# Layer values between the MLP's second products, later exps and work moved off VectorE, in a fused two-layer graph kernel

## The chip, the cores and the metric

The kernel runs on one core of one Trainium2 chip. The metric is the device time of one execution in microseconds (us). Instructions of a core are issued by five engines: TensorE (PE in the profile; its weight loads are shown apart as PEld), VectorE (DVE), ScalarE (ACT), GpSimd (POOL) and SyncE (SP), which issues most of the DMAs. In this kernel the order of each engine's instructions is fixed when the program is built, and an engine waits at the first instruction whose inputs or buffers are not ready.

## What is computed

Sixteen graphs (batches) of 1024 nodes with 256 features go through two layers. `adj` is symmetric with ones on its diagonal.

```python
# layer 0: attention over neighbours (8 heads of 32, q = k = v), then an MLP
h = relu(layernorm(x))
n = layernorm(h) * gamma1 + beta1                # split into 8 heads
p = softmax(where(adj > 0, n @ n.T / sqrt(32), -inf))
h = h + p @ n
y = layernorm(h) * gamma2 + beta2
x = x + h + gelu(y @ W1 + b1) @ W2 + b2
# layer 1: one head over neighbours
f = relu(layernorm(x));  g = f @ W
e = leaky_relu((g @ a_1).T + g @ a_2 + (g @ a_12) @ g.T, 0.2)
a = softmax(where(adj > 0, e, -9e15))
x = x + elu(f @ W_1 + (a @ f) @ W_2)
```

## The kernel before

**Two chains at once.** The Python code that builds the program runs several generators ("streams") against a common scale of places and always advances the one that is furthest behind. Stream A is the attention of batch b. Stream B is everything after the attention of batch b−1: MLP, layer 1 and the store. The other streams prepare the next batch: C loads and normalizes it, M loads masks, K compares masks, P makes the first MLP inputs. Each stream's instructions thus land between the others', on every engine in the same order.

**Stream A.** For b > 0 a batch has 24 units, numbered 0 to 23 here. A unit is one key tile (128 keys) for one group of four heads and one half (512) of the queries. `scores` makes the scores of the four heads (TensorE, `s`, L994), adds the mask on VectorE in two instructions of 128x1024 (L1007), and takes the exps on ScalarE in four instructions of 128x512 that also sum their rows (`weights`, L1014). `go_on` then lets TensorE multiply the exps of the unit before with the values (`weigh`, `o`, L1109), and adds 2.0 to the planner's clock. Units 0 to 15 are for the first half of the queries; in every second one (the even ones) `mirror` also transposes the exps (VectorE, L1030), writes them to DRAM and adds up their columns on GpSimd (`add_up`, L1043), so that units 16 to 23 can read the mirrored blocks back instead of computing them (`weigh_mirrored`, L1091). The first two heads' exps are issued in `scores`, the other two after `go_on`.

**Deferred work.** `defer(us, f)` puts an instruction aside until the planner's clock has moved on by `us`; `run_deferred`, called after every step of a stream, issues what is due, in order of due time. The clock is an estimate of TensorE time: 2.0 for a unit, 0.5 for a transpose to PSUM ("turn"), 1.75 or 0.9 for a piece of stream B.

**Turns.** `ask(turn, c)` puts a turn into a list; `make_turns` issues what is in the list ahead of the next unit. `wait_for(turn, c)` holds stream B until that turn has been issued.

**Stream B.** It is cut into pieces of 1.75 (some 0.9) clock units, some three to a unit of A, in this order: `expand(0)`; the last attends of the batch before; `expand(1)`, `contract(0)`, `expand(2)`, `contract(1)`, `expand(3)`, `contract(2)`, `contract(3)`; then layer 1. Here c = 0..3 is a chunk of 256 nodes, two tiles of 128. `expand` is the MLP's first product (TensorE `ph`, ScalarE `hid` L1303, four pieces) and `contract` its second (TensorE `po`, added to the rows by VectorE, L1327; four pieces, two for each tile). `prepare1` takes a finished chunk's statistics (VectorE `st_d`, L741 to L744, then GpSimd `rs_d`, L746) and defers its normalization (`ft`, VectorE L750) by 5.0; `turn1` issues that normalization if it has not been issued yet, transposes the chunk (`ptf`, L1349) and lets ScalarE write it into `fT` (L1352). Layer 1 then has `project_half` (`puT`, evicted by ScalarE, L1364), `values` (`pg`, one for each of 8 tiles, evicted into `gw` by ScalarE for even tiles and VectorE for odd ones, L1379), `weights` (`lg`, VectorE L1397 and L1402, ScalarE exp L1403) and `attend` (`pf`, `pa`).

**Buffers.** All PSUM results of stream B and all turns go through one ring of three banks, `psm`. A `po` tile stays open over its two pieces. The outputs `o` of the attention have a single bank, `pso`. The scores have two pairs of banks.

**Normalizations.** `normalize` (L750, VectorE) is called for the attention's values (`nrm`), for the MLP's input (`y`, in `prepare`) and for layer 1 (`ft`). The output `o` of a unit group is copied out of PSUM by VectorE (`os`, L1118).

Of the kernel before, what the change touches and what calls it, by code (L numbers as in the profile page):

```python
# [495 lines left out]
def fast_path(  # L496
# [28 lines left out]
    nc = tc.nc  # L525
# [10 lines left out]
    TPH = QW // P  # L536
# [209 lines left out]
        nc.gpsimd.tensor_tensor(rs, ve, mhalf[:, :nt], op=ALU.pow)  # L746
        return mv, rs

    def normalize(dst, src, mv, rs, t):
        nc.vector.tensor_scalar(  # L750
            dst, src, mv[:, t, 0:1], rs[:, t : t + 1], op0=ALU.subtract, op1=ALU.mult
        )

# [5 lines left out]
    def defer(us, f):  # L759
        deferred.append((clock[0] + us, len(deferred), f))  # L760

        return clock[0] + us
# [13 lines left out]
    def prologue(b, st):  # L776
# [33 lines left out]
        def value(i):  # L810
            mv, rs = stats["b", i]
            for j in range(TPC):
                t = i * TPC + j
                nrm = tmpp.tile([P, D], F32, tag="w1", bufs=6, name=f"nrm_{b}_{t}")
                normalize(nrm, h[t // TPH][:, t % TPH, :], mv, rs, j)
                nc.gpsimd.tensor_mul(nrm, nrm, g1)
                nc.gpsimd.tensor_add(va[:, t, :], nrm, be1)

# [149 lines left out]
    def attention(b, st):  # L968
# [9 lines left out]
        def scores(qh, g, kt):  # L978
            qs = slice(qh * QW, (qh + 1) * QW)
            sc = [  # L980
                psc.tile([P, 2, QW], F32, tag=f"sc{i}", name=f"s_{b}_{g}_{qh}_{kt}_{i}") for i in range(2)
            ]

            by_pe = 2 if b == 0 else 0
            if by_pe:
                for j in range(by_pe):
                    matmul(
                        sc[j // 2][:, j % 2, :], ident8, st[qh][:, kt // 2, :, kt % 2], start=True, stop=False
                    )
                clock[0] += 0.45  # L990
            for j in range(GH):
                r = slice(j * HD, (j + 1) * HD)
                for c in range(0, P, P // 2):
                    nc.tensor.matmul(  # L994
                        sc[j // 2][c : c + P // 2, j % 2, :],
                        kT[r, g, kt * P + c : kt * P + c + P // 2],
                        kT[r, g, qs],
                        start=j >= by_pe,
                        stop=True,
                    )  # L1000
            mb = st[qh][:, kt // 2, :, kt % 2].unsqueeze(1).to_broadcast([P, 2, QW])
            es = []
            for i in range(2):
                e = ep.tile([P, 2, QW], F32, tag="e", name=f"e_{b}_{g}_{qh}_{kt}_{i}")
                masked = sc[i]
                if 2 * i >= by_pe:
                    nc.vector.tensor_tensor(e, masked, mb, op=ALU.add)  # L1007
                    masked = e
                es.append(e)

                def weights(e=e, masked=masked, i=i):
                    for j in range(2):
                        n = 2 * i + j
                        nc.scalar.activation(  # L1014
                            e[:, j], masked[:, j], AF.Exp, scale=SCALE,
                            accum_out=sums[kt // TPH, g][:, n, kt % TPH, qh : qh + 1],
                        )

                if i == 0:
                    weights()  # L1020
            return es, weights


        def mirror(g, kt, es):
            x = xp.tile([P, NT // 2 * GH, GH, HD], F32, tag="x", name=f"x_{b}_{g}_{kt}")
            if g not in blocks:
                blocks[g] = dramp.tile([NT // 2 * GH, NT // 2 * GH, HD, P], F32, tag=f"blocks{g}", name=f"blocks_{b}_{g}")

            def turn(i):
                nc.vector.transpose(  # L1030
                    x[:, :, 2 * i : 2 * i + 2, :].rearrange("p c h j -> p h c j"),
                    es[i].rearrange("p h (c i) -> p h c i", i=HD),
                )

            def write():
                for a in range(GH):
                    nc.sync.dma_start(
                        blocks[g][(kt - TPH) * GH + a].rearrange("c i e -> i c e"),
                        x[a * HD : (a + 1) * HD].rearrange("p c h j -> p c (h j)"),
                    )  # L1040

            def add_up():
                add = lambda out, p, q: nc.gpsimd.tensor_tensor(out, p, q, op=ALU.add)  # L1043
                part = denp.tile([P, TPH * GH, GH, 8], F32, tag="part", bufs=1, name=f"part_{b}_{g}_{kt}")
                add(part, x[:, :, :, 0:8], x[:, :, :, 8:16])
                add(part, part, x[:, :, :, 16:24])
                add(part, part, x[:, :, :, 24:32])
                add(part[:, :, :, :4], part[:, :, :, :4], part[:, :, :, 4:])
                add(part[:, :, :, :2], part[:, :, :, :2], part[:, :, :, 2:4])
                row = denp.tile([P, GH, TPH, GH], F32, tag="row", name=f"row_{b}_{g}_{kt}")  # L1050
                add(
                    row.rearrange("p a t h -> p t a h"),
                    part[:, :, :, 0].rearrange("p (t a) h -> p t a h", a=GH),
                    part[:, :, :, 1].rearrange("p (t a) h -> p t a h", a=GH),
                )
                if ("rows", g) not in blocks:
                    blocks["rows", g] = dramp.tile([TPH, P, GH * TPH * GH], F32, tag=f"rows{g}", name=f"rows_{b}_{g}")
                defer(7.0, lambda: nc.sync.dma_start(blocks["rows", g][kt - TPH], row.rearrange("p a t h -> p (a t h)")))

            defer(1.5, lambda: turn(0))  # L1060
            defer(3.5, lambda: turn(1))
            defer(5.5, write)
            defer(6.5, add_up)

        def gather(g):
            r = blocks["sums", g] = denp.tile([P, NT // 2 * GH, TPH * GH], F32, tag="sums", bufs=1, name=f"gather_{b}_{g}")
# [37 lines left out]
        def weigh(qh, g, kt, es, first, last):  # L1104
            if first and not (mirrored and qh == 1):
                acc[g, qh] = pso.tile([P, QW], F32, tag="o", name=f"o_{b}_{g}_{qh}")
            o = acc[g, qh]
            for j in range(GH):
                nc.tensor.matmul(  # L1109
                    o[j * HD : (j + 1) * HD, :],  # L1110
                    va[:, kt, (g * GH + j) * HD : (g * GH + j + 1) * HD],
                    es[j // 2][:, j % 2, :],
                    start=first and not (mirrored and qh == 1),
                    stop=last,
                )
            if last:
                c = os[g, qh] = tmpp.tile([P, QW], F32, tag="w2", bufs=5, name=f"os_{b}_{g}_{qh}")
                nc.vector.tensor_copy(c, o)  # L1118
                if qh == NQH - 1:
                    close(qh, g)  # L1120

# [88 lines left out]
    def prepare(b, st, c):  # L1210

        h = hs[b]
        assert finished[b, c // 2] == NG
        ts = range(c * TPC, (c + 1) * TPC)
        mv, rs = norm_stats([h[t // TPH][:, t % TPH, :] for t in ts], f"c{b}_{c}")

        def apply():
            y = tmpp.tile([P, TPC, D], F32, tag="y", name=f"y_{b}_{c}")
            for i, t in enumerate(ts):
                normalize(y[:, i, :], h[t // TPH][:, t % TPH, :], mv, rs, i)  # L1220
            st["y", c] = y, None

        st["y", c] = None, defer(5.0, apply)
# [8 lines left out]
    def rest(b, st, tails):  # L1232
# [4 lines left out]
        def load(c):  # L1237
            for t in range(c * TPC, (c + 1) * TPC):
                xt.append(xbp.tile([P, D], F32, tag="xb", name=f"xb_{b}_{t}"))
                nc.sync.dma_start(xt[t], rows(x, b, t))  # L1240
# [180 lines left out]
        def attend(t, es):  # L1421
# [32 lines left out]
            defer(14.0, lambda: nc.sync.dma_start(rows(out, b, t), z))  # L1454
            yield 1.75, True

        load(0)
        ask(turn, 0)
        yield
# [18 lines left out]
        prepare1(1)  # L1478
        fT = st["fT"] = midp.tile([P, DC, N], F32, tag="mid1", name=f"fT_{b}")
        ask(turn1, 0)  # L1480
        yield from contract(2, hid[2])
        prepare1(2)
        ask(turn1, 1)
        yield from contract(3, hid[3])
        uT = midp.tile([P, DC, N], F32, tag="mid2", name=f"uT_{b}")
        prepare1(3)
        ask(turn1, 2)
# [1 line left out]
        def some_values(*ts):  # L1489
            for t in ts:  # L1490
                values(t, fT)
                yield 0.9, t % 2 == 1
# [11 lines left out]
        yield from wait_for(turn1, 0)  # L1504
        yield from wait_for(turn1, 1)
        yield from project_half(0, 0)
        yield from some_values(0, 1)
        if b < B - 1:
            ask(turn1, 3)
        yield from project_half(0, 1)  # L1510
        yield from some_values(2, 3)
        if b == B - 1:
            ask(turn1, 3)
        yield from wait_for(turn1, 2)
        yield from some_values(4, 5)
        yield from some_weights(0, 0, 1)
        yield from wait_for(turn1, 3)
        yield from project_half(1, 0)
        yield from project_half(1, 1)
        yield from some_values(6, 7)  # L1520

        before = None
        for c in range(NCH):
# [186 lines left out]
```

## Time and profile before

| what | us |
|---|---|
| median of three runs (3427.57 to 3433.45) | 3429.52 |
| the profiled execution's own time | 3435.34 |
| its span, first to last instruction | 3433.2 |
| ScalarE busy, mean over the span | 1966.2 (57%) |
| one batch in the middle: from the first unit of one batch (1608.9) to that of the next (1818.7) | 209.8 |
| exps of a unit on ScalarE, unit 0 of that batch (1613.76 to 1616.33) | 2.57 |
| a piece of stream B with 32 matmul records, spacing in the timeline | 1.73 |
| scores and weighting of a unit on TensorE | 1.04 and 1.00 |

A busy share is an average over the span, and stages differ. All batches but the first and the last have the same order, so one batch in the middle stands for them; a wait that occurs 14 times in the list of waits is one that each such batch has. Times of the timeline are us from the span's start.

### The profile page before, as it was taken

To read this page: it belongs to the slowest core of one execution; us is meant where nothing else is said; L and a number is where in the kernel's file an instruction comes from. 1 tells how busy PE (TensorE), PEld (TensorE's weight loads), DVE (VectorE), ACT (ScalarE), POOL (GpSimd) and SP (SyncE) were. 2 spreads that over 40 slices of the span, in tenths; PEclk is the share of its full clock that TensorE was granted. 3 is DMA by queue.
4 is the path that set the end of the run, shared out by engine and by line. 5 is a ranking of instruction groups with operands and counts; after the bars stand their busy time and mean duration, and the time that the engine had idled before them with its cause. 6 is when DMAs were issued, how large, how long until landed. Compare 5 with 4: busy or idle time off the path is not lost. (4 is left out here: it accounts for less than half of the span.)

```text
span 3433.2 us, 114690 instructions
## 1 busy us (share of the span) xinstructions
PE 3239.3 (94%) x48866; PEld 1590.8 (46%) x48866; DVE 2791.5 (81%) x5201; ACT 1966.2 (57%) x4744; POOL 1535.2 (45%) x1758
## 2 busy tenths in 40 slices
PE   6899999999999999999999999999999999999998
PEld 1344444444444444444444444444444444444477
DVE  6788888888888888887888888888888888887844
ACT  6765745647456474655646556475564745646442
POOL 3553553535535254462545526355353554525220
PEclk9999999999999999999999999999999999999999
DMA  5245455464555545555454555545546445554510
GB/s 134 58 115 157 94 121 125 114 158 99 133 121 122 140 109 121 127 120 144 113 134 112 122 138 119 139 109 125 126 113 158 99 121 132 116 143 101 132 38 14
DMA packets 741158, 404.81 MB, mean 118 GB/s; under 512 B 173216, under 2 KB 699936, under 8 KB 740640
## 3 DMA queue, kind: packets, MB, share of 16 engines
q1 hardware_dynamic: 740352, 397.14, 47.9%
q8 instruction: 386, 6.32, 0.8%
q14 instruction: 132, 1.08, 0.1%
q10 hardware_dynamic: 288, 0.26, 0.0%
HBM read 233.97 MB, written 146.54 MB: 111 GB/s over the span
## 5 line engine op out<-in xcount | busy, mean ns | idle before, releaser
L1014 ACT ACTIVATE e<-e 128x512 f32<-128x512 f32 x1504 | 928.5, 619 | 839.7 <-DVE e L1007 837.5
L1007 DVE TENSOR_TENSOR e<-s,mk 128x1024 f32<-128x1024 f32 x752 | 885.1, 1216 | 204.1 <-PE s L994 197.5
L574 PE MATMUL ph<-yT,w 128*32 128x256 f32 x7808 | 445.8, 379 | 16.4 <-DVE yT L1279 15.0
L574 PE MATMUL pa<-gw,e 128*32 128x258 f32 x7584 | 446.4, 380 | 9.1 <-DVE e L1397 9.1
L574 PE MATMUL lg<-fT,uT 128*32 128x256 f32 x7680 | 452.3, 380 | 0.0
L994 PE MATMUL s<-kT 32*64 32x512 f32 x6272 | 447.0, 622 | 1.1 <-DVE e L1007 1.1
L574 PE MATMUL po<-w,hid 128*32 128x256 f32 x7680 | 434.4, 379 | 0.0
L1109 PE MATMUL o<-e,va 128*32 128x512 f32 x3136 | 428.8, 614 | 1.4 <-ACT e L1014 1.4
L574 PEld LDWEIGHTS ph<-yT,w 128*32 128x32 f32 x7808 | 250.4, 110 | 220.2 <-DVE yT L1279 32.5
L574 PEld LDWEIGHTS po<-w,hid 128*32 128x32 f32 x7680 | 250.0, 110 | 202.7 <-issue 48.5
L574 PEld LDWEIGHTS lg<-fT,uT 128*32 128x32 f32 x7680 | 248.5, 110 | 200.2 <-issue 29.7
L574 PEld LDWEIGHTS pa<-gw,e 128*32 128x32 f32 x7584 | 247.5, 110 | 196.0 <-issue 22.1
L1043 POOL TENSOR_TENSOR part<-part,x 128x512 f32<-128x512 f32 x240 | 309.3, 1289 | 18.8
L1030 DVE STREAM_TRANSPOSE x<-e 128x1024 f32<-128x1024 f32 x240 | 291.5, 1232 | 9.9 <-ACT e L1014 8.2
L966 POOL TENSOR_TENSOR h<-h,ot 128x512 f32<-128x512 f32 x64 | 82.1, 1282 | 455.3 <-DVE ot L962 455.3
L1397 DVE SCALAR_TENSOR_TENSOR e<-lg,gw,mk 128x256 f32<-128x256 f32 x512 | 222.9, 476 | 72.3 <-PE lg L574 62.3
L1014 ACT ACTIVATION_READ_ACCUMULATOR e<-e 128x1 f32 x1504 | 281.1, 187 | 0.0
L1403 ACT ACTIVATE e<-e,shift 128x512 f32<-128x512 f32 x256 | 183.1, 716 | 150.8 <-DVE e L1402 141.1
L1303 ACT ACTIVATE hid<-ph,b1c 128x256 f32<-128x256 f32 x512 | 203.6, 465 | 83.7 <-PE ph L574 61.3
L1043 POOL TENSOR_TENSOR part<-x 128x512 f32<-128x512 f32 x120 | 155.3, 1294 | 208.6 <-DVE x L1030 151.2
L919 POOL TENSOR_TENSOR odd<-mk,mq 128x512 bf16<-128x512 fp8e5 x192 | 236.2, 1237 | 20.9 <-DVE uneven L926 18.7
L1109 PEld LDWEIGHTS o<-e,va 128*32 128x32 f32 x3136 | 63.2, 108 | 327.4 <-issue 212.8
(143 smaller groups left out, 4380.4 us busy)
## 6 DMA issues: line engine op xcount, KB each, us to landing
blocks<-x SPq DMA_DIRECT2D x480, 256.0 KB, 4.7
em<-blocks SPq DMA_DIRECT2D x240, 512.0 KB, 5.0
adj<-in_adj_dram SPq DMA_DIRECT2D x248, 256.0 KB, 4.1
h<-in_x_dram SPq DMA_DIRECT2D x64, 256.0 KB, 4.2
xb<-in_x_dram SPq DMA_DIRECT2D x128, 128.0 KB, 3.4
out_dram<-z SPq DMA_DIRECT2D x128, 128.0 KB, 4.1
rows<-row SPq DMA_DIRECT2D x120, 32.0 KB, 2.6
gather<-rows SPq DMA_DIRECT2D x120, 32.0 KB, 3.3
```

The source lines that it names most:

```text
L574: nc.tensor.matmul(out[c : c + HD], lhsT[:, c : c + HD], rhs, start=start, stop=stop)
L919: nc.gpsimd.tensor_tensor(odd.rearrange("p (u v x) -> p u v x", u=2, v=2), key.rearrange("p (u v x) -> p u v x", u=2, v=2), query.rearrang ...
L966: nc.gpsimd.tensor_add(ho, ho, ot.rearrange("p t j d -> p t (j d)"))
L994: nc.tensor.matmul(sc[j // 2][c : c + P // 2, j % 2, :], kT[r, g, kt * P + c : kt * P + c + P // 2], kT[r, g, qs], start=j >= by_pe, stop= ...
L1007: nc.vector.tensor_tensor(e, masked, mb, op=ALU.add)
L1014: nc.scalar.activation(e[:, j], masked[:, j], AF.Exp, scale=SCALE, accum_out=sums[kt // TPH, g][:, n, kt % TPH, qh : qh + 1],)
L1030: nc.vector.transpose(x[:, :, 2 * i : 2 * i + 2, :].rearrange("p c h j -> p h c j"), es[i].rearrange("p h (c i) -> p h c i", i=HD),)
L1043: add = lambda out, p, q: nc.gpsimd.tensor_tensor(out, p, q, op=ALU.add)
L1109: nc.tensor.matmul(o[j * HD : (j + 1) * HD, :], va[:, kt, (g * GH + j) * HD : (g * GH + j + 1) * HD], es[j // 2][:, j % 2, :], start=first ...
L1303: nc.scalar.activation(hid[:, f0 + i, :], ph[:, i, :], AF.Identity, bias=b1c[:, f0 + i : f0 + i + 1])
L1397: nc.vector.scalar_tensor_tensor(e[:, j, :], lg[:, j, :], gw[:, kt, D : D + 1], st[c // 2][:, kt // 2, qs, kt % 2], op0=ALU.add, op1=ALU.add,)
L1403: ready = defer(2.5, lambda: nc.scalar.activation(e, e, AF.Exp, bias=shift))
```

## The change

- `normalize` gets an argument for its engine. The attention's values (`nrm`, for b > 0) and the MLP's input (`y`) are normalized by GpSimd instead of VectorE; `ft` stays on VectorE.
- For b > 0 all four exps of a unit are deferred by 2.5 in the planner's clock instead of being issued in and right after `scores`. A unit advances the clock by 2.0, so they come after the next piece of stream B and what this piece issues on ScalarE. In `mirror` the due times of the transposes, the write and the sums go up by 1.9 to 2.1.
- The copy `os` goes from VectorE to ScalarE.
- The `values` of tiles 0 and 1 are issued inside `contract(2)`, each after a tile's two pieces, those of tiles 2 and 3 inside `contract(3)`. Layer 1's start is ordered anew: the two first `project_half` follow each other, and the values of tiles 4 to 7 stand singly between `weights` and `project_half`.

```diff
-    def normalize(dst, src, mv, rs, t):
-        nc.vector.tensor_scalar(
+    def normalize(dst, src, mv, rs, t, engine=nc.vector):
+        engine.tensor_scalar(
             dst, src, mv[:, t, 0:1], rs[:, t : t + 1], op0=ALU.subtract, op1=ALU.mult
         )
...
-                normalize(nrm, h[t // TPH][:, t % TPH, :], mv, rs, j)
+                normalize(nrm, h[t // TPH][:, t % TPH, :], mv, rs, j, nc.gpsimd if b else nc.vector)
...
-                if i == 0:
+                if b > 0:
+                    defer(2.5, weights)
+                elif i == 0:
                     weights()
-            return es, weights
+            return es, weights if b == 0 else lambda: None
...
-            defer(1.5, lambda: turn(0))
-            defer(3.5, lambda: turn(1))
-            defer(5.5, write)
-            defer(6.5, add_up)
+            defer(3.6, lambda: turn(0))
+            defer(5.4, lambda: turn(1))
+            defer(7.4, write)
+            defer(8.5, add_up)
...
-                nc.vector.tensor_copy(c, o)
+                nc.scalar.copy(c, o)
...
-                normalize(y[:, i, :], h[t // TPH][:, t % TPH, :], mv, rs, i)
+                normalize(y[:, i, :], h[t // TPH][:, t % TPH, :], mv, rs, i, nc.gpsimd)
...
+        def with_values(pieces, c):
+            for i, piece in enumerate(pieces):
+                yield piece
+                if i % 2 == 1:
+                    yield from wait_for(turn1, c)
+                    values(c * TPC + i // 2, st["fT"])
+                    yield 0.9, i // 2 == 1
...
-        yield from contract(2, hid[2])
+        yield from with_values(contract(2, hid[2]), 0)
         prepare1(2)
         ask(turn1, 1)
-        yield from contract(3, hid[3])
+        yield from with_values(contract(3, hid[3]), 1)
...
         yield from project_half(0, 0)
-        yield from some_values(0, 1)
         if b < B - 1:
             ask(turn1, 3)
         yield from project_half(0, 1)
-        yield from some_values(2, 3)
         if b == B - 1:
             ask(turn1, 3)
         yield from wait_for(turn1, 2)
-        yield from some_values(4, 5)
-        yield from some_weights(0, 0, 1)
+        yield from some_values(4)
+        yield from some_weights(0, 0)
+        yield from some_values(5)
+        yield from some_weights(0, 1)
         yield from wait_for(turn1, 3)
         yield from project_half(1, 0)
+        yield from some_values(6)
         yield from project_half(1, 1)
-        yield from some_values(6, 7)
+        yield from some_values(7)
```

## The prediction

> **What bounds the kernel now.** I read the page's busy table first, then who TensorE waits for, then one batch in time order, then the windows of its stages.
>
> ```profile
> PE 3239.3 (94%) x48866; PEld 1590.8 (46%) x48866; DVE 2791.5 (81%) x5201; ACT 1966.2 (57%) x4744; POOL 1535.2 (45%) x1758
> ```
>
> TensorE is the bound: the span is its 3239.3 us and 194 us of waits. The change takes no matmul away, so only the waits can go. From the list of waits of TensorE (total us, times, longest):
>
> ```profile
> PE ptf L1349 <- ACT uT L1364: 26.1, 14, 1.9
> PE o L1091 <- DMA em<-blocks: 22.9, 19, 2.3
> PE pg L574 <- ACT gw L1379: 20.6, 14, 1.5
> PE ptk L824 <- POOL va L817: 20.5, 6, 15.5
> PE pg L574 <- ACT uT L1364: 18.7, 15, 1.3
> PE ptk L824 <- ACT uT L1364: 18.4, 14, 1.3
> PE ph L574 <- DVE yT L1279: 15.0, 12, 2.0
> ...
> PE o L1091 <- DVE os L1118: 10.2, 13, 0.8
> PE pa L574 <- DVE e L1397: 9.1, 14, 0.7
> ```
>
> Four of these, 26.1 + 20.6 + 18.7 + 18.4 = 83.8 us, are one place in each of 14 batches, the start of layer 1. The timeline of TensorE shows it:
>
> ```profile
> 1712.85 2.22 PE L574 MATMUL pg<-wo,fT 128*32 128x258 f32 x32 [1.48 <-ACT gw L1379]
> 1716.94 0.66 PE L1349 MATMUL ptf<-ident,ft 128*128 128x128 f32 x4 [1.86 <-ACT uT L1364]
> 1717.52 1.11 PE L994 MATMUL s<-kT 32*64 32x512 f32 x16
> ...
> 1732.48 1.08 PE L574 MATMUL pg<-wo,fT 128*32 128x258 f32 x16 [1.30 <-ACT uT L1364]
> 1734.88 0.63 PE L824 MATMUL ptk<-ident,va 128*128 128x128 f32 x4 [1.32 <-ACT uT L1364]
> ```
>
> A `pg` takes 0.86 us and a bank of the ring of three, so a pair of them runs the ring round before ScalarE, busy with exps, has emptied it: 1.48 + 1.86 us up to unit 13 (its scores are the third line), 1.30 + 1.32 up to unit 15, together 5.96. The stages, from unit 0 to 9, 9 to 13, 13 to 15, and 15 to the next batch:
>
> ```profile
> 1608.90:1681.50 72.60, 71.31 (x1165) 35.05 (x1164) 59.19 (x90) 50.88 (x118) 41.80 (x49) 1.00 0.39 85
> 1681.50:1717.50 36.00, 32.33 (x472) 14.86 (x468) 33.50 (x78) 21.41 (x49) 19.38 (x24) 1.00 0.62 144
> 1717.50:1735.40 17.90, 15.28 (x213) 6.22 (x212) 15.74 (x26) 9.81 (x25) 12.64 (x14) 1.00 0.41 78
> 1735.40:1818.70 83.30, 79.81 (x1303) 40.09 (x1303) 68.44 (x136) 39.35 (x101) 25.00 (x28) 1.00 0.65 162
> ```
>
> Columns after the length: busy us of PE, PEld, DVE, ACT, POOL. What matters is the second row: in those 36.00 us VectorE is busy for 33.50, more than TensorE's 32.33. The average of 81% hides that. This is exactly where the change puts the `values`.
>
> [...] `ft` on VectorE has median 411 ns and maximum 1446, and two of them from 1701.18 took 2.44 us while GpSimd ran `part`. [...] no row here shows a one-input tensor_scalar on GpSimd. From above it is bounded by the two-input rows of that size, 0.885 (`nrm`) and 0.742 (`va`). I take 0.65[...].
>
> **Part by part.**
>
> *Normalizations.* These groups leave VectorE (mean ns, total us):
>
> ```profile
> L750 DVE TENSOR_SCALAR y<-h,mv_c,rs_c 128x256 f32<-128x256 f32 x128 | 92.2, 763 | 0.1
> ...
> L750 DVE TENSOR_SCALAR nrm<-h,mv_b,rs_b 128x256 f32<-128x256 f32 x128 | 47.9, 416 | 2.7 <-POOL rs_b L746 2.6
> ...
> L1118 DVE COPY os<-o 128x512 f32<-128x512 f32 x64 | 43.5, 680 | 0.6 <-PE o L1109 0.6
> ```
>
> VectorE loses 92.2 + 120 x 0.416 + 43.5 = 186 us; GpSimd gains 248 x 0.65 = 161 us[...], going from 45% to 50%. Neither is TensorE's time by itself. `nrm` (10 us or more ahead of its `ptk`) and `y` of chunks 0, 1, 3 have slack. The tight one is chunk 2: its `y` may queue behind `add_up` (5.9 us, here 1640.54 to 1646.4) and end near 1648; its transposes run at 1649.7. Cost 0, up to 1.5 us a batch if a mask comparison (1.24) gets in between.
>
> *`os` on ScalarE.* The unit that ends a group has its mask additions (2.35 us) ahead of `os` on VectorE; on ScalarE nothing is left in front of it, since the exps of the unit before are done. The 0.8 us wait of `o` L1091 goes: 10.2 / 14 = -0.73 a batch. ScalarE gains 64 x about 0.67 (the 128x512 `uT` row), hidden in its 43% idle time.
>
> *Later exps.* After a unit's start: scores 1.04, weighting 1.00, a piece 1.73, its eviction 0.84, exps 2.57 make 7.2 us. The weighting that needs them begins no earlier than the shortest unit distance, 7.2, plus 1.04. Margin 1.1 us; the GELU (4.5 us with both table loads) is due at 3.0, after the exps at 2.5, so it stays behind them. Cost 0, at most 1 us a batch. Its own gain is 0 too: the waits above on ScalarE are all in the stage that is rebuilt anyway. What counts is the shift of the transposes: those of unit 8 were both ahead of unit 9's masks; now the second (due 7.4 after unit 8's start; the clock at unit 9 is 7.25) comes behind them, 1.23 us of VectorE more in the full stage.
>
> *Values and the new order.* A unit of A passes for each 5.32 of stream B's 134 clock units (25.2 widths a batch). `contract(2)` begins at B's 50.8, 0.30 of a unit after unit 9. Counting pieces from there, stream B now issues: before unit 10 two halves of `po`; then pg, po, po, pg, po; unit 11: po, pg, po; unit 12: po, pg, puT, puT; unit 13: pg, lg, pg, lg; unit 14: puT, pg, puT; unit 15: pg, lg, lg. No two `pg` follow each other, and after unit 13 I find every bank free in time: in the worst place, before the `pg` of tile 7, the copy of tile 6 ends about half a us early. So the 1.30 + 1.32 go.
>
> Before unit 13 it is different. `turn1` of chunks 2 and 3 both fall ahead of unit 13 (both asked for after unit 12), and the second forces `ft` of chunk 3 onto VectorE at once. Its chain starts at the last `po`: add, statistics, `rs_d`, `ft`. TensorE has only pg 0.86 + puT 1.72 + puT 1.72 + ptf 0.58 = 4.9 us to fill; before it was over 12 us (1702.5 to 1716.94), of which VectorE took 11 (`ft` was done at 1713.6). So VectorE's whole queue from unit 9 to this `ft` now ends before unit 13 can begin. It was 33.50 us of work plus 1.4 us of small gaps from 1682.63 on. It loses a pair of `nrm` (-0.64), gains the transposes of unit 8 (+1.23), and I add 0.8 for idling where a shorter lead makes it wait on TensorE (`ptos` of unit 12, between 0 and 1.7). `ft` ends at 1682.63 + 33.50 + 1.4 + 0.59 + 0.8 = 1718.9, unit 13 starts 0.3 later, 1719.2 against 1717.52: +1.7 us, for the same amount of stream B done. On the way the stalls show as `po` and `puT` waiting for a bank (a `po` that closes one `pg`, 0.86 us, before its bank is needed again) and `ptf` waiting for `ft`. From both sides: +0.9 with no extra idling; +5 if mask conversions and `ft` meet GpSimd's longer queue at each collision (1.7 us for the pair seen at 1701) with full idling.
>
> *Sum a batch:* +1.7 - 2.62 - 0.73 = -1.65; fourteen batches -23 us. The last batch's tail has no units beside it; its early turn costs under 1 us. 3435.34 becomes 3412; the median of the runs lies 5.8 below the profiled one, so 3429.5 becomes 3407.
>
> **Rivals.**
> *Full gain (0.17).* VectorE, 186 us lighter, keeps up, and all of the 83.8 + 10.2 us goes: 3335. For it: the average. Against: only 0.64 of the 186 us leave the stage that is full.
> *Slower (0.28).* The chain into chunk 3's `ft` is longer than reckoned[...]: GpSimd runs `add_up`, then normalizations, while VectorE converts masks and makes `ft`. It decides from the point where unit 13 comes over 3.35 us later than before (2.62 + 0.73). At +5 each batch loses 1.65, +23 us: 3453. For it: 2.44 us for two `ft`. Against: GpSimd is busy 19.38 of the 36 us, so it has room.
> *The exps do harm or nothing.* A weighting that waits for its exps would show as `o` L1109 behind `e` L1014 (1.4 us in all now). I hold it inside the other cases.
>
> **How the numbers follow.** Forecast 0.55, its own range 3380 to 3435; full gain 0.17, slower 0.28. The range 3355 to 3455 leaves out most of the full gain and the far end of the slower case. A measurement of this kernel tells 0.2%, 7 us, from no change. The forecast's case is faster by more with 0.74, the same with 0.16, slower with 0.10. Faster: 0.55 x 0.74 + 0.17 = 0.58; same: 0.09 and 0.02 of the slower case, 0.11; slower 0.31.
>
> **What would show it.** Right: `pg` waits on `gw` and `uT` nearly gone; `o` L1091 on `os` gone; in their place `ptf` on VectorE's `ft`, and `po` or `puT` on VectorE's `xb`, some 4 us a batch; VectorE near full from unit 9 to 13, near 76% in the mean; `o` L1109 on `e` still near zero. Wrong: no new waits of TensorE on VectorE (full gain), or `pty` waiting for GpSimd's `y`, or weightings waiting for exps.

## The result and the profile after

| | before | after |
|---|---|---|
| median of the runs, same chip, us | 3428.77 | 3519.42 |
| ratio, 95% interval | 1 | 1.0262 (1.0246 to 1.0279) |
| span of the profiled execution, us | 3433.2 | 3519.4 |
| its mean granted TensorE clock | 0.993 | 0.982 |

The changed kernel is 91 us slower. From its page, the busy line:

```profile
PE 3276.0 (93%) x48866; PEld 1617.3 (46%) x48866; DVE 2674.6 (76%) x4889; ACT 2001.1 (57%) x4808; POOL 1854.3 (53%) x2006
```

TensorE has the same 48866 matmuls, yet is busy for 36.7 us longer (3239.3 before): some of them run slower. VectorE lost 117 us, not the 186 that were reckoned, and GpSimd gained 319, not 161. Who TensorE waits for after the change (total us, times, longest):

```profile
PE ptf L1351 <- DVE ft L750: 57.7, 30, 4.8
PE o L1093 <- DMA em<-blocks: 31.9, 35, 2.6
PE puT L574 <- DVE xb L1329: 24.5, 13, 2.0
PE ptk L824 <- POOL va L817: 24.2, 6, 15.8
PE pa L574 <- DVE e L1399: 23.9, 16, 1.7
PE ptos L960 <- DVE xb L1329: 19.0, 14, 1.4
...
PE lg L574 <- DVE e L1399: 7.6, 13, 0.6
...
PE o L1111 <- ACT e L1014: 2.2, 1, 2.2
```

(Lines after L1016 stand two higher than before.) The waits of `pg` and `ptk` on ScalarE's `gw` and `uT`, 83.8 us, are gone. In their place stand `ptf` on `ft`, `puT` and `ptos` on `xb`: 101.2 us, all on VectorE, all ahead of unit 13. The weightings do not wait for the later exps (last line). One batch in the order of time, TensorE (start, duration, in brackets the wait before it):

```profile
1749.14 0.65 PE L960 MATMUL ptos<-ident,os 128*128 128x128 f32 x4 [1.43 <-DVE xb L1329]
...
1758.02 1.92 PE L574 MATMUL puT<-fT,wm 128*32 128x512 f32 x16 [1.88 <-DVE xb L1329]
1759.88 0.66 PE L1351 MATMUL ptf<-ident,ft 128*128 128x128 f32 x4
1763.78 0.48 PE L1351 MATMUL ptf<-ident,ft 128*128 128x128 f32 x2 [3.25 <-DVE ft L750]
1764.95 0.69 PE L1351 MATMUL ptf<-ident,ft 128*128 128x128 f32 x2 [0.69 <-DVE ft L750]
1765.57 2.01 PE L994 MATMUL s<-kT 32*64 32x512 f32 x16
1767.51 1.94 PE L1111 MATMUL o<-e,va 128*32 128x512 f32 x8
1769.22 1.84 PE L574 MATMUL pg<-wo,fT 128*32 128x258 f32 x16
```

`ptf` of chunk 3 waits 3.25 us for its `ft`, as the slower case of the prediction had it. The lines below it show what no case had: unit 13's scores take 2.01 us (1.11 at other units), its weighting 1.94 (1.07), `pg` 1.84 (1.05). Windows of the same batch; columns: length, busy us of PE, PEld, DVE, ACT, POOL, granted clock (the share of TensorE's full speed), DMA share, GB/s. The rows are the stages from unit 9 to 13, 13 to 15, 15 to the next batch, and 0 to 9:

```profile
1724.83:1765.57 40.74, 32.89 (x473) 14.95 (x469) 37.99 (x78) 22.75 (x54) 25.54 (x29) 0.98 0.51 122
1765.57:1782.24 16.67, 16.67 (x197) 6.17 (x196) 11.58 (x20) 7.91 (x21) 10.76 (x13) 0.84 0.32 69
1782.24:1868.01 85.77, 81.10 (x1313) 41.90 (x1312) 68.58 (x128) 42.44 (x109) 37.25 (x37) 1.00 0.62 157
1652.55:1724.83 72.28, 71.08 (x1162) 35.11 (x1161) 51.36 (x82) 50.64 (x116) 45.70 (x52) 1.00 0.40 90
```

Around the 3.25 us wait, TensorE alone, in stretches of 3.41 us (length, busy us, granted clock, DMA share, GB/s):

```profile
1757.16:1760.58 3.42, 2.51 (x20) 1.00 0.53 163
1760.58:1763.99 3.41, 0.21 (x2) 1.00 0.00 0
1763.99:1767.40 3.41, 2.72 (x20) 0.50 0.79 162
1767.40:1770.82 3.42, 3.42 (x32) 0.50 0.86 188
1770.82:1774.23 3.41, 3.41 (x68) 1.00 0.24 48
```

After a stretch in which TensorE worked for 0.21 us, its clock is halved for two stretches, 6.83 us: it is still at half after one with 2.72 us of work, and full again after one with 3.42. TensorE was not idle for a whole stretch each time: the paragraph "When the clock drops" below shows a halving after a stretch with 1.48 us of work.

Stage lengths as the mean of the 14 middle batches, from the starts of the units' scores, against the prediction's terms. The `pg` of tile 7 (0.87 us) now stands behind unit 15's start instead of ahead of it; the last column is corrected for it:

| stage | before | after | forecast | slower rival | measured |
|---|---|---|---|---|---|
| 0 to 9 | 71.90 | 71.93 | 0 | 0 | +0.03 |
| 9 to 13 | 36.18 | 41.00 | +1.7 | +5 | +4.82 |
| 13 to 15 | 18.76 | 16.31 | -2.62 | -2.62 | -1.58 |
| 15 to next | 83.05 | 86.08 | -0.73 | -0.73 | +2.16 |
| batch | 209.90 | 215.31 | -1.65 | +1.65 | +5.41 |

Fourteen times 5.41 is 76 of the span's 86 us; the other 10 are outside these batches.

So three questions: what fills VectorE up to unit 13, what the half clock costs, and where the 2.16 after unit 15 come from. VectorE's and then GpSimd's timeline in that stage:

```profile
1746.42 2.33 DVE L594 TENSOR_SCALAR mq<-adj 128x512 fp8e5<-128x512 int32 x2
...
1755.82 1.81 DVE L594 TENSOR_SCALAR mq<-adj 128x512 fp8e5<-128x512 int32 x2
...
1759.69 1.25 DVE L1032 STREAM_TRANSPOSE x<-e 128x1024 f32<-128x1024 f32 x1
...
1762.10 1.24 DVE L1032 STREAM_TRANSPOSE x<-e 128x1024 f32<-128x1024 f32 x1
1763.26 1.63 DVE L750 TENSOR_SCALAR ft<-xb,mv_d,rs_d 128x256 f32<-128x256 f32 x2
```

```profile
1745.76 2.70 POOL L1045 TENSOR_TENSOR part<-part,x 128x512 f32<-128x512 f32 x2
...
1750.18 1.23 POOL L750 TENSOR_SCALAR nrm<-h,mv_b,rs_b 128x256 f32<-128x256 f32 x1
...
1755.84 1.51 POOL L966 TENSOR_TENSOR h<-h,ot 128x512 f32<-128x512 f32 x1
```

Two pairs of mask conversions (L594) take 2.33 and 1.81 us where the median of one is 0.42: each pair runs beside GpSimd instructions that read two tiles (2.70 and 1.51 us in the timeline above). The rest of the trace of the changed kernel agrees: the 99 conversions that no GpSimd instruction overlaps take 428 ns at most, the 61 that only the mirror's sums (L1045) overlap take 852 in the mean. Both transposes of a unit stand ahead of the `ft` that TensorE waits for. L594 alone on VectorE, unit 9 to 13 (length, busy us, clock, DMA share, GB/s), before:

```profile
1681.48:1717.52 36.04, 2.79 (x6) 1.00 0.62 143
```

and after:

```profile
1724.83:1765.57 40.74, 5.10 (x6) 0.98 0.51 122
```

In the same way the transposes go from 4.90 to 6.36, the small `ve` (L744) from 1.62 to 2.29, and L750 falls from 4.55 to 4.09. These make +2.31 + 1.46 + 0.67 - 0.46 = 3.98 of the 4.49 by which VectorE's work in the stage grew (33.50 to 37.99). VectorE's idle time there hardly changed, 2.54 and 2.75. From the groups of the changed kernel (total us, mean ns):

```profile
L750 POOL TENSOR_SCALAR nrm<-h,mv_b,rs_b 128x256 f32<-128x256 f32 x120 | 168.5, 1404 | 0.0
L750 POOL TENSOR_SCALAR y<-h,mv_c,rs_c 128x256 f32<-128x256 f32 x128 | 161.1, 1269 | 1.6
L594 DVE TENSOR_SCALAR mq<-adj 128x512 fp8e5<-128x512 int32 x248 | 141.6, 608 | 7.7 <-DMA adj<-in_adj_dram 7.5
L816 POOL TENSOR_TENSOR nrm<-nrm,g 128x256 f32<-128x256 f32 x128 | 96.0, 750 | 11.1 <-DVE nrm L750 1.1
```

A normalization on GpSimd takes 1.27 to 1.40 us, longer than a two-input product of the same size (0.75).

### The profile page after: what moved, and what is told of

Same layout as the page of the kernel before. It is cut to its first block, busy times and chain, and to the rows that moved or that the text cites. A ratio compares the mean times of both kernels' runs of the same rounds, so it can differ in the third digit from the quotient of the medians.

```text
span 3519.4 us, 114617 instructions
## 1 busy us (share of the span) xinstructions
PE 3276.0 (93%) x48866; PEld 1617.3 (46%) x48866; DVE 2674.6 (76%) x4889; ACT 2001.1 (57%) x4808; POOL 1854.3 (53%) x2006
## 5 line engine op out<-in xcount | busy, mean ns | idle before, releaser
L574 PE MATMUL pa<-gw,e 128*32 128x258 f32 x7584 | 446.9, 380 | 24.6 <-DVE e L1399 23.9
L994 PE MATMUL s<-kT 32*64 32x512 f32 x6272 | 457.9, 633 | 3.6 <-DVE e L1007 3.6
L574 PE MATMUL po<-w,hid 128*32 128x256 f32 x7680 | 444.6, 380 | 0.0
L1111 PE MATMUL o<-e,va 128*32 128x512 f32 x3136 | 437.6, 626 | 2.2 <-ACT e L1014 2.2
L574 PEld LDWEIGHTS lg<-fT,uT 128*32 128x32 f32 x7680 | 255.8, 111 | 201.2 <-issue 24.8
L574 PEld LDWEIGHTS pa<-gw,e 128*32 128x32 f32 x7584 | 250.5, 110 | 210.1 <-issue 53.5
L1045 POOL TENSOR_TENSOR part<-part,x 128x512 f32<-128x512 f32 x240 | 317.8, 1324 | 18.8
L1045 POOL TENSOR_TENSOR part<-x 128x512 f32<-128x512 f32 x120 | 153.4, 1278 | 179.8 <-DVE x L1032 179.8
```

The source lines that it names most:

```text
L574: nc.tensor.matmul(out[c : c + HD], lhsT[:, c : c + HD], rhs, start=start, stop=stop)
L994: nc.tensor.matmul(sc[j // 2][c : c + P // 2, j % 2, :], kT[r, g, kt * P + c : kt * P + c + P // 2], kT[r, g, qs], start=j >= by_pe, stop= ...
L1111: nc.tensor.matmul(o[j * HD : (j + 1) * HD, :], va[:, kt, (g * GH + j) * HD : (g * GH + j + 1) * HD], es[j // 2][:, j % 2, :], start=first ...
```

## The experiments

Ahead of each result stand the ranges that its theories gave before it ran. All ratios are to the kernel before, timed on the same chip. Experiments 1 to 8, 12, 13 and 15 begin from the changed kernel, 9 to 11 and 14 from the one before. "Lock theory" is the author's name for an estimate: that what VectorE loses beside a busier GpSimd, as in the conversions above (852 ns in the mean beside the sums, 428 at most beside nothing), makes the loss. The traces show the longer instructions; why they are longer is not shown.

### The forced turn, the normalizations, the exps and the order: one undone at a time

`e1_turn_later`, chunk 3's turn asked for one unit later:

```diff
         yield from project_half(0, 0)
-        if b < B - 1:
-            ask(turn1, 3)
         yield from project_half(0, 1)
...
         yield from some_values(4)
+        if b < B - 1:
+            ask(turn1, 3)
         yield from some_weights(0, 0)
```

> The changed kernel with one edit: chunk 3's turn is asked for after the values of tile 4 instead of between the two first project_half, so that it falls ahead of unit 14 and not of unit 13. Turn theory (the loss is the normalization ft of chunk 3 forced in front of unit 13, and the half clock that follows TensorE's idling there): the 3.25 + 0.69 us of ptf behind ft and about 3.3 us of half clock a batch go, 15 batches: 3519 falls to 3410 to 3430, granted clock back to 0.99. Lock theory (GpSimd's normalizations of 1.23 us each stretch VectorE's mask conversions and ft): the waits on xb (1.43 and 1.88) stay and VectorE's queue is as long, so at most half of the loss goes: 3465 to 3490. Exps theory (the moved transposes fill VectorE): as the lock theory.

`e2_norms_on_vector`, `nrm` and `y` back on VectorE:

```diff
-                normalize(nrm, h[t // TPH][:, t % TPH, :], mv, rs, j, nc.gpsimd if b else nc.vector)
+                normalize(nrm, h[t // TPH][:, t % TPH, :], mv, rs, j)
...
-                normalize(y[:, i, :], h[t // TPH][:, t % TPH, :], mv, rs, i, nc.gpsimd)
+                normalize(y[:, i, :], h[t // TPH][:, t % TPH, :], mv, rs, i)
```

> The changed kernel with nrm and y normalized by VectorE again. Lock theory: VectorE's busy time from unit 9 to 13 falls from 37.99 us to about 35, ptf waits under 1.5 us for ft, most batches keep the full clock: 3430 to 3460. Turn theory: the chain into ft is as long as TensorE's cover is short, and nrm's 0.64 us comes back; ptf still waits 2 us or more and the clock still drops: 3485 to 3520.

`e3_exps_at_once`, exps and the mirror's due times as before:

```diff
-                if b > 0:
-                    defer(2.5, weights)
-                elif i == 0:
+                if i == 0:
                     weights()
...
-            defer(3.6, lambda: turn(0))
+            defer(1.5, lambda: turn(0))
```

(and so on for the mirror's other three; both parts stand whole below).

> The changed kernel with the exps issued at once and the mirror's due times as before. Exps theory: 1.23 us of transposes leave VectorE's full stretch and it no longer waits 54.9 us in all for exps: 3440 to 3470. Turn and lock theories: the forced ft is still late; 1.2 us a batch at most, 3495 to 3520; ScalarE's evictions behind exps may bring back some waits for uT.

`e4_old_order` takes back `with_values` and all of layer 1's new start:

```diff
-        yield from with_values(contract(2, hid[2]), 0)
+        yield from contract(2, hid[2])
...
-        yield from with_values(contract(3, hid[3]), 1)
+        yield from contract(3, hid[3])
...
         yield from project_half(0, 0)
+        yield from some_values(0, 1)
```

> The changed kernel with stream B's order of before (no values inside contract, values in pairs); exps, os and normalizations stay changed. Turn theory: everything lost goes and os stays gained: 3405 to 3430. Lock theory: pa and lg still wait for VectorE's e (23.9 + 7.6 us against 9.1 before) and the four waits at layer 1's start come back longer: 3440 to 3470.

| run | median us | ratio (95%) | 9 to 13, us | 13 to 15 | 15 to next |
|---|---|---|---|---|---|
| changed | 3519.42 | 1.0262 (1.0246 to 1.0279) | 41.00 | 16.31 | 86.08 |
| e1 turn later | 3458.53 | 1.0092 (1.0072 to 1.0112) | 35.81 | 17.53 | 85.61 |
| e2 norms on VectorE | 3472.67 | 1.0128 (1.0111 to 1.0145) | 40.20 | 15.77 | 84.16 |
| e3 exps at once | 3440.65 | 1.0036 (1.0024 to 1.0047) | 37.84 | 15.70 | 83.76 |
| e4 old order | 3468.76 | 1.0113 (1.0096 to 1.0130) | 38.42 | 15.77 | 86.13 |

(In e4 the `pg` of tile 7 stands ahead of unit 15, as before; in the others behind its start.) Each gives back 47 to 79 us. Added they would be 237 us, of a loss of 91: the parts share one loss. One thing that they share can be read from the pages: TensorE's busy time falls by 33, 23, 35 and 20 us from the changed kernel's 3276.0, with the same matmuls, and the mean granted clock of the profiled runs is 0.992, 0.988, 0.991 and 0.986 against 0.982. So part of each gain is the full clock coming back, which can be won only once. e1 and e2 came out between the ranges of their theories: neither the turn alone nor what VectorE loses beside GpSimd alone is the loss. e3 came out as the exps theory has it and e4 as the lock theory.

e1 moves one instruction's due place and 9 to 13 falls below its length before. Part of this is chunk 3's turn, which now stands behind the start of unit 13. From 9 to 15 together it is 53.34 us, against 57.31 in the changed kernel and, less the `pg` of tile 7, 54.07 before: the wait of `ptf` on `ft` is a matter of where the turn is forced. e2 hardly helps there; most of its gain lies after unit 15. e3 gives the most, but it is two edits in one: when the exps are issued, and when the mirror's transposes and sums are.

### The exps and the mirror's due times apart

`e5_mirror_as_before`:

```diff
-            defer(3.6, lambda: turn(0))
-            defer(5.4, lambda: turn(1))
-            defer(7.4, write)
-            defer(8.5, add_up)
+            defer(1.5, lambda: turn(0))
+            defer(3.5, lambda: turn(1))
+            defer(5.5, write)
+            defer(6.5, add_up)
```

`e6_exps_at_once_mirror_late`:

```diff
-                if b > 0:
-                    defer(2.5, weights)
-                elif i == 0:
+                if i == 0:
                     weights()
-            return es, weights if b == 0 else lambda: None
+            return es, weights
```

> The changed kernel with the mirror's four due times as before (1.5, 3.5, 5.5, 6.5), exps still deferred. Transpose theory (the loss undone by issuing exps at once is that the shifted transposes land in VectorE's full stretch and in front of layer 1's additions): 3435 to 3460, as with exps at once. Exps theory (the later exps themselves hold VectorE's queue, since the transposes wait for them): 3490 to 3525, and VectorE's wait of x for e grows from 54.9 us.

> The changed kernel with exps issued at once, the mirror's later due times kept. Transpose theory: the loss stays, 3490 to 3520, as the transposes are where they were. Exps theory: the transposes find finished exps and the loss goes: 3435 to 3460.

On the changed kernel, median us (ratio):

| | mirror's old times | mirror's late times |
|---|---|---|
| exps at once | e3: 3440.65 (1.0036) | e6: 3550.18 (1.0348, 1.0331 to 1.0365) |
| exps later | e5: 3461.22 (1.0085, 1.0065 to 1.0104) | changed: 3519.42 (1.0262) |

The late times cost 110 us with the exps at once and 58 with the later ones. The later exps cost 21 with the old times and save 31 with the late ones. (e5 ended 1 us above the range of the transpose theory; e6 lies above both ranges.)

Why the sign turns can be read from the lists of waits, added up by the engine that TensorE waits for. With the old times the later exps take 21.0 us of waits on ScalarE away (53.6 to 32.6), and add 31.8 on VectorE (84.7 to 116.5) and 10.6 of busy time. With the late times they take 53.5 on ScalarE away (77.9 to 24.4), and add only 15.2 on VectorE (137.7 to 152.9), 5.1 on DMAs and 2.1 of busy time. The large waits on ScalarE in e6 are 26.4 us for `os` and 23.3 for `fT` (16.1 and 9.4 in e3). What stood ahead of these two in ScalarE's queue was not traced.

The stage from unit 9 to 13 in e3, columns as above:

```profile
1685.40:1722.80 37.40, 32.26 (x472) 14.83 (x468) 33.76 (x76) 21.52 (x50) 23.13 (x28) 1.00 0.56 143
```

and in e6:

```profile
1739.00:1780.20 41.20, 32.61 (x472) 14.86 (x468) 38.06 (x78) 23.90 (x56) 25.27 (x29) 1.00 0.48 121
```

The third busy column is VectorE's: 33.76 and 38.06 for the same stream B, and the length follows it, +4.30 and +3.80. Of these 4.30, 1.25 are mask conversions (3.85 and 5.10) and 1.41 transposes (4.95 and 6.36). In e5 the exps come late and the times are old: conversions 3.85, transposes 6.25. So it is the late times, not the later exps, that lengthen the conversions further; an added transpose comes with either edit. After unit 15 the mean is 83.76 and 83.59 with the old times (e3, e5), 86.27 and 86.08 with the late ones (e6, changed).

### Each part alone on the kernel before

Each adds one part of the change's diff, as it stands there, to the kernel before: `e9_exps_alone` the exps with the mirror's due times; `e10_values_alone` stream B's new order; `e11_norms_alone` the normalizations on GpSimd; `e14_mirror_late_alone` the due times only:

```diff
-            defer(1.5, lambda: turn(0))
-            defer(3.5, lambda: turn(1))
-            defer(5.5, write)
-            defer(6.5, add_up)
+            defer(3.6, lambda: turn(0))
+            defer(5.4, lambda: turn(1))
+            defer(7.4, write)
+            defer(8.5, add_up)
```

> The kernel before with only the exps' part of the change (exps deferred by 2.5, mirror's due times later). Stretch theory (whatever lands in VectorE's full stretch from unit 9 to 13 or moves GpSimd's sums onto its mask conversions costs time, in stream B's old order too): 3450 to 3480. Turn theory (the part costs only where a turn waits for ft): 3420 to 3435.

> The kernel before with only stream B's new order. Turn theory: the four waits of 5.96 us a batch go, ptf's wait for ft of about 3 us and those of puT and po for xb come: 3440 to 3465. If VectorE kept up: 3345 to 3400.

> The kernel before with only nrm and y on GpSimd. Lock theory: conversions and ft meet a busier GpSimd and VectorE's uneven waits longer for odd: 3435 to 3455. Relief theory (as the 19 us between the two runs with exps at once and the later turn): 3405 to 3422.

> The kernel before with only the mirror's four due times later, exps at once. Transpose theory: most of the 41 us of the exps' part alone, 3450 to 3490. Exps theory: 3425 to 3440.

| run | median us | ratio (95%) |
|---|---|---|
| e9 exps and due times | 3471.88 | 1.0125 (1.0109 to 1.0140) |
| e10 new order | 3453.76 | 1.0064 (1.0049 to 1.0080) |
| e11 normalizations | 3426.07 | 0.9989 (0.9979 to 0.9999) |
| e14 due times only | 3492.52 | 1.0183 (1.0166 to 1.0200) |

The due times are the dearest edit of the change, some 63 us alone; with the later exps it is some 42, so here too the later exps save time beside the late times. e9 and e10 lie in the ranges of the stretch and of the turn theory, e14 2.5 us above that of the transpose theory, and e11 between its two. The new order alone is slower too: its TensorE waits 44.6 us, 15 times, for `ft`, as forced there as in the changed kernel. Waits of TensorE in e14:

```profile
PE o L1091 <- DVE os L1118: 44.1, 15, 3.3
PE ptf L1349 <- DVE xb L1327: 40.3, 15, 2.9
```

The first was 10.2 before. VectorE's timeline in e14 around unit 15:

```profile
1763.58 1.25 DVE L1030 STREAM_TRANSPOSE x<-e 128x1024 f32<-128x1024 f32 x1
...
1768.32 2.35 DVE L1007 TENSOR_TENSOR e<-s,mk 128x1024 f32<-128x1024 f32 x2 [1.79 <-PE s L994]
1770.59 1.23 DVE L1030 STREAM_TRANSPOSE x<-e 128x1024 f32<-128x1024 f32 x1
```

The second transpose of unit 14 now stands behind the masks of unit 15 (third line), in a queue that runs without a pause until `os` at 1783.13. In the kernel before both stood ahead of those masks, where VectorE then had 2.14 us of idle time. From unit 15 to the next batch e14 is 85.93 us long in the mean, 2.88 more than before.

### `os` on ScalarE

`e15_changed_os_on_vector`:

```diff
-                nc.scalar.copy(c, o)
+                nc.vector.tensor_copy(c, o)
```

> The changed kernel with os on VectorE again. With deferred exps nothing stands in front of os on ScalarE, and its wait is 0.8 us in all; on VectorE it stands behind the mask additions and what is late there: 10 to 45 us come back as o L1091 on os: 3530 to 3560. If os on ScalarE gains nothing: 3505 to 3522.

Measured 3519.67 (1.0271, 1.0246 to 1.0295) against 3519.42, as if `os` on ScalarE gained nothing. TensorE's wait for `os` comes back, 21.5 us, and the time does not change; the waits on `em` and on VectorE's `e` (`pa`) are 6.8 and 3.4 us shorter there. So taking the wait for `os` away gained nothing, as others grew; those two are 10.2 of the 21.5 us, and the rest was not traced.

### The half clock

Theory: the idle time ahead of unit 13 costs more than itself, since the matmuls after it run at half speed (unit 13's scores 2.01 us against 1.11). `e13_fill_the_wait` gives TensorE eight matmuls, whose result nothing reads, in the bank that chunk 3's transposes overwrite:

```diff
             pt = ps_tile([P, DC, CW], f"ptf_{b}_{c}")
+            if c == 3 and b < B - 1:
+                for _ in range(8):
+                    matmul(pt[:, 0, :], wm[:, 0, :P], wm[:, 1, :])
```

> The changed kernel with 8 matmuls of 128x256 (0.43 us each) issued into the bank of chunk 3's ptf ahead of its transposes; they compute nothing that is used. TensorE waits 3.25 + 0.69 us there for ft anyway, so they cost nothing if the wait stays. Clock theory (the idling itself is what brings the half clock for some 6.6 us, worth 3.3 us a batch): the clock stays full, 3470 to 3485 instead of 3519. If the half clock has another cause: 3512 to 3530.

Measured 3482.31 (1.0155, 1.0138 to 1.0172), as the clock theory has it: more work, 37 us less time. TensorE's timeline in e13 around the start of unit 13 (the fill is the first line):

```profile
1740.05 3.66 PE L574 MATMUL ptf<-wm 128*32 128x256 f32 x64
1743.64 0.44 PE L1354 MATMUL ptf<-ident,ft 128*128 128x128 f32 x2
1744.55 0.44 PE L1354 MATMUL ptf<-ident,ft 128*128 128x128 f32 x2 [0.47 <-DVE ft L750]
1744.92 1.11 PE L994 MATMUL s<-kT 32*64 32x512 f32 x16
1745.96 1.07 PE L1111 MATMUL o<-e,va 128*32 128x512 f32 x8
```

Scores 1.11 and weighting 1.07 again. The stage 9 to 13 is as long as in the changed kernel (40.82 and 41.00), where VectorE was busy for 37.99 of 40.74 us; 13 to 15 goes from 16.31 to 14.17, the batch from 215.31 to 212.55. So the fill gives back 2.8 us a batch, 37 us in all. Not all of this came with the change: in 8 of the 14 batches of the kernel before, unit 13 also ran at the half clock, and its stage from 13 to 15 is 17.91 us at the full clock and 18.76 in the mean. Less these 0.85 us a batch, my estimate is that some 25 of the 91 us are what the change added in half clock.

### Towards a faster version

`e7_at_once_turn_later` is e1's and e3's edits together; `e8_at_once_turn_later_vector` adds e2's, `e12_best_os_on_vector` adds e15's to e7.

> The changed kernel with exps at once, the mirror's old due times and chunk 3's turn asked for after the values of tile 4; values inside contract, os and the normalizations stay changed. Both single undoings together: ptf no longer waits 3.0 us a batch for ft, about 1.5 us of the new wait for a bank that lg holds comes in its place: 3415 to 3430. If the two undoings had removed the same loss (the half clock), 3435 to 3445.

> As the run before, with nrm and y on VectorE again: what is left of the change is os on ScalarE and the values inside contract. Lock theory: VectorE's conversions and ft are short again, 3395 to 3415. If the 186 us taken off VectorE are worth more[...]: slower than the run before.

> The run with exps at once and the later turn (3424), with os on VectorE again. There o L1091 waited 16.1 us in all for os on ScalarE, which stands behind exps that are gated by the mask additions; before it waited 10.2 for os on VectorE. So 3415 to 3422; if the 43 us more on VectorE cost as much, 3420 to 3432.

| run | median us | ratio (95%) |
|---|---|---|
| e7 | 3423.59 | 0.9980 (0.9970 to 0.9991) |
| e8 | 3442.38 | 1.0036 (1.0022 to 1.0050) |
| e12 | 3412.08 | 0.9947 (0.9934 to 0.9961) |

e7 came out as expected; e8 refutes the lock theory for this kernel, and e12 is 3 us below its range. Here the normalizations gain 19 us on GpSimd (e7 against e8), where in the changed kernel they cost 47 (e2). What decides is not shown: VectorE's wait for GpSimd's `odd` grows with them in both (25.8 to 63.2 us from e8 to e7, 44.1 to 86.3 from e2 to the changed kernel). `os` on ScalarE costs 11.5 us here (e7 against e12). TensorE's wait for it is 16.1 us on ScalarE and 13.7 on VectorE; with `os` on VectorE the 7.6 us that `ph` waits for ScalarE's `hid` are gone too, and TensorE is busy for 4.4 us less. e12 beats both kernels. Its busy line:

```profile
PE 3225.2 (95%) x48866; PEld 1590.7 (47%) x48866; DVE 2734.8 (80%) x4953; ACT 1958.0 (57%) x4744; POOL 1859.0 (55%) x2006
```

Its stage 9 to 13 is 33.95 us (36.18 before), and its mean clock 0.997: the matmuls take 14 us less than in the kernel before.

## Why the prediction was wrong

**Right.** The 83.8 us of waits on ScalarE went, and the pieces of stream B came in the order that was counted out. The new waits are those named: `ptf` on `ft`, `puT` and a bank on `xb`. `y` of chunk 2 does not hold `pty`, and the exps hold no weighting. That VectorE's queue up to chunk 3's `ft` decides when unit 13 begins is shown by the wait of 3.25 us and by e1, where it goes.

**The failing step** is the term for that queue: "It loses a pair of `nrm` (-0.64), gains the transposes of unit 8 (+1.23)", net +0.59, and from it +1.7 us to unit 13. VectorE's work grew by 4.49 and the stage by 4.82. The mechanism was right and the term mis-sized. The transposes were nearly as costed (+1.46), and of the 0.8 for idling 0.21 came. What was costed at nothing is that VectorE's other instructions get longer beside a GpSimd that is busier and runs its sums at another time: the mask conversions (+2.31), the small statistics (+0.67; in the changed kernel the 46 `ve_b` that a GpSimd instruction overlaps take 457 ns in the mean, the 18 others 171 at most). Of the conversions' part, 1.25 belong to the late due times: e6 against e3 shows it with everything else equal. The rest is there with the old times too; with the late times, 0.98 of the conversions' time goes when the normalizations go back to VectorE (4.12 in e2). The prediction had seen this (the conversions that only GpSimd's sums overlap take 852 ns in the mean, against 428 at most alone), but it read it from `ft` alone and put it into the upper end only. A moved due time moves every instruction behind it; only VectorE's were counted. This term is 3.12 of the 7.06 us a batch by which the forecast missed. With it right and the others as forecast the sum would be +1.47 a batch, 3450 us; 1.04 more are missing between unit 13 and 15, and 2.89 after unit 15.

**GpSimd's normalization** was taken at 0.65 us, an estimate of the author's that no row of the kernel before showed; it takes 1.27 to 1.40 in the mean. The two-input rows (0.742 and 0.885) were no upper bound. Alone this costs nothing (e11), in the changed kernel 47 us (e2), of which 23 are TensorE's busy time. 1.9 of e2's 3.3 us a batch lie after unit 15. VectorE waits there for GpSimd's part of the mask comparison (`uneven` on `odd`, in the whole span 33.6 us before, 86.3 after, 44.1 in e2). That this wait is the cause is not shown: it is 62.5 us in e11 too, where nothing is lost.

**The gain of 2.62 between unit 13 and 15** was there: without the half clock (e13) the stage is 14.17, which for equal work is 2.87 less than the 17.91 of the batches before that had the full clock. With the half clock 1.58 remain, against the mean before. The prediction priced the new wait at its length; that TensorE's clock drops after it was in no case.

**After unit 15** 0.73 was to be gained by `os` and 2.16 was lost. The wait for `os` did go, but `pa` and `lg` wait longer for VectorE's `e` (9.1 to 23.9 us and none to 7.6, 1.6 a batch) and the mirrored weighting for `em` (22.9 to 31.9, 0.6 a batch); `os` back on VectorE changes nothing (e15). The stage belongs to the late due times: with the old ones it is 2.5 us shorter (e5), and they alone lengthen it by 2.88 on the kernel before (e14). With the late times the second transpose of unit 14 starts 3.43 us into unit 15, behind its masks; in e5 it starts 0.22 us into it, ahead of them. That this one place is the whole cause was not tested.

**The slower rival** had the place, the longer chain into `ft` and the delay (+5 against 4.82), but held the two other terms fixed, which made 3453 of what was 3519. The later exps, thought free, cost 21 us with the mirror's old times (e3 against e5) and save 31 with the late ones (e6 against the changed kernel).

**When the clock drops.** The waits of 1.48 and 1.86 us ahead of unit 13 are in every middle batch of the kernel before, but only 8 of the 14 got the half clock. Two of these batches, TensorE alone, in the columns used for it above; the first keeps its clock and the second loses it:

```profile
1711.75:1715.17 3.42, 2.16 (x32) 1.00 0.35 92
1715.17:1718.58 3.41, 1.64 (x22) 1.00 0.51 136
1718.58:1721.99 3.41, 3.41 (x64) 1.00 0.89 201
1919.96:1923.38 3.42, 1.94 (x28) 1.00 0.02 3
1923.38:1926.79 3.41, 1.48 (x25) 1.00 0.48 153
1926.79:1930.20 3.41, 3.41 (x24) 0.50 0.82 173
```

In each of the 17 traces of this case the clock changes only at whole multiples of 3.413 us from its other changes (from 130 us on to 20 us before the end, to within 5 ns), so these stretches have fixed borders. Counting all of them from 230 us on: the clock was halved 224 times, each time at the end of a stretch in which TensorE was busy for 1.55 us or less (once 1.78), and it stayed full after 15452 stretches with 1.42 us or more. It came back after stretches with 3.01 us or more, and stayed at half after 56 with 3.06 or less. In the trace of the changed kernel alone there are 19 halvings, after 1.45 us of work or less (once 1.78), and 909 stretches with 1.53 us or more after which the clock stayed full; in that of the kernel before 10, after 1.55 or less, and 912 with 1.59 or more. So in the two batches above the same wait cost a halving or not by where the borders lay. In the second batch the wait of 1.86 us falls whole into one stretch, which leaves 1.48 us of work there; in the first 0.09 us of it fall into the stretch before, which leaves 1.64.

**Open.** Why the normalizations on GpSimd cost time in the changed kernel and gain some in e7; and what part of the 2.16 us after unit 15 each of the three longer waits has.

## What to carry to other kernels

When a due time is moved, list what every engine issues because of it, and ask what GpSimd is doing at VectorE's new place (here a conversion beside GpSimd's sums took 852 ns in the mean, 428 at most beside nothing). From unit 9 to 13 VectorE was 93% busy both before (33.50 of 36.00 us) and after (37.99 of 40.74), and an `ft` forced there held TensorE for 3.25 us: e1 moved one turn by a unit and got back 61 us. Price a TensorE wait like these 3.25 us with the slow matmuls that may follow it (6.83 us at half the clock); if it can't go, filling it with unused matmuls may be worth its cost (e13 was 37 us faster with them).

## What the runs showed of the hardware

- TensorE's clock was halved, and came back, only at borders whole multiples of 3.413 us apart. It was halved after such a stretch with at most 1.55 us of work (once 1.78), so in the kernel before a wait of 1.86 us was enough where it fell whole into one (1.48 us of work left). In e13 eight unused matmuls of 0.46 us each prevented it ahead of unit 13 (its scores took 1.11 us again), 2.8 us a batch.
- A normalization of 128x256 with two per-partition scalars took at least 1.215 us on GpSimd in the changed kernel, against 0.41 in the median on VectorE (0.32 at best), and was longer than GpSimd's two-input products (0.75 in the mean).
- A mask conversion of 128x512 on VectorE took 0.42 to 0.43 us in the changed kernel where no GpSimd instruction overlapped it. Where only the mirror's sums on GpSimd did, it took 0.85 in the mean and 1.51 at most; where only a normalization on GpSimd did, 0.51 in the mean and 0.71 at most. Its mean over all went from 518 ns in the kernel before to 608.
